# Latent attention on one core: full-column products issued as four 32-column tiles, transposes put last in each step

## The chip, the cores and the metric

The kernel runs on one core of one Trainium2 chip. The metric is device time in microseconds (us), as the median of several runs. Engines are named as in the profile: PE is the matrix engine, PEld its weight loads, DVE the vector engine, ACT the scalar engine, POOL GpSimd, SP the engine that issues most DMAs.

## What is computed

The input is 8 sequences of 1024 tokens with 256 features, all in float32. A latent attention comes first, then a feed-forward part of two layers of windowed attention and gated MLP; the change touches only the first. Cut to that, the reference is:

```python
# NH=16 heads of HD=16, DR=32 rope features, latent width D_C=128
x = layernorm(x)
c_kv   = x @ W_kv_down                        # 256 -> 128
k_rope = rotary(c_kv @ W_k_rope)              # 32, shared by the heads
k, v   = c_kv @ W_k_up, c_kv @ W_v_up         # 256 each
q      = x @ W_q
q_rope = rotary(x @ W_q_rope)
scores = (einsum(q, k) + einsum(q_rope, k_rope)[:, None]) / sqrt(HD + DR)
w      = softmax(causal(scores))
out    = x0 + (w @ v) @ W_o                   # x0: the input before layernorm
```

## The kernel before

**Tiling.** `mla` handles the 8 batches (sequences) one after another. Four heads are worked on together, as a group g of four 32-row slices of the array. The 512 queries of one half c against 128 keys kb of one group make a unit; small causal units are put together in pairs. There are 36 units in each batch, and the loop that starts at L545 (`mla`) takes one unit in each step, so a batch has 36 steps, numbered 0 to 35 below.

**One step.** In a step the loop does, in this order:

- `scores` (L391) of this step's unit. Its products have 32 rows and 128 columns of the array each (K=32), into two PSUM tiles `sc` of a pool with two buffers; then two exponentials on ACT (L407) turn them into `pt`.
- `turned` (L411) of the unit of the step before: two DVE multiplications (L421) by the exponential of the shared rope scores, `er`.
- `values` (L423) of the unit of two steps before. Its products have 128 rows and 32 columns (four heads side by side in four column tiles), into `acc`.
- `finished` (L444) if a group ended in the step before: four 128x128 transposes into `pst`, then a reciprocal and a product on DVE (L449, L450).
- `do(b, step)` (L529): what the table at L487 puts beside this step. These are the dense work of the next batch (normalising, `turn`, `down`, `rope_q`, `rope_k`, `query`, `keys`, `value`, `rotary`) and the end of this or the former one (`out_turn`, `out_add`). Entries read (step, whose batch, what).

**Shapes on the array.** All dense products go through `times` (L182) with all 128 rows and 128 columns; all transposes go through `flip` (L185), also 128x128. So PE works in three forms: 32x128 for scores, 128x32 for values, 128x128 for the rest. A float32 product shows as two matmul records and two weight loads in the trace.

**Order and buffers.** Inside `tc.manual_schedule` (L546) PE, DVE, ACT and POOL take their instructions in the order in which the program writes them. The results of `times` and `flip` share a PSUM pool `psum1` with two buffers (L167, tag `mm`); a result is read out by ACT or DVE, and its buffer then comes free. `query`, `down`, `rope_q` and `out_add` hold their buffer over two steps, since each step makes one half of the sum.

**After it.** The windowed attention (`local`, L577) begins when the last batch is done. Its loads are issued while the last batch still runs.

The loop around the change is:

```python
                    if done:
                        bt, e = done.pop(0)
                        bt.finished(*e)
                    done += ended
                    do(b, step)
```

Of the kernel before, what the change touches and what calls it, by code (L numbers as in the profile page):

```python
# [81 lines left out]
def preln_mla_local_kernel(  # L82
# [27 lines left out]
    nc = tc.nc  # L110
# [44 lines left out]
    def mla(ctx: ExitStack, verdict):  # L155
# [23 lines left out]
            return xt  # L179


        def times(out, w, rhs, start, stop):  # L182
            nc.tensor.matmul(out, w, rhs, start=start, stop=stop)  # L183

        def flip(out, t):  # L185
            nc.tensor.transpose(out, t, ident)
# [61 lines left out]
        class Batch:  # L248
# [51 lines left out]
            def dense(self, name, ws, rhs, n, c):  # L300

                if c == 0:
                    self.sums[name, n] = psum.tile([P, 512], F32, tag="mm", name=f"{name}{self.b}_{n}")
                ps = self.sums[name, n]
                times(ps, ws[c], rhs[c][:, HALF[n]], c == 0, c == len(ws) - 1)
                return self.sums.pop((name, n)) if c == len(ws) - 1 else None
# [43 lines left out]
            def value(self, g):  # L350
                self.v = vs[self.b % 2]
                ps = psum.tile([P, 512], F32, tag="mm", name=f"psv{self.b}_{g}")
                for i in range(2):
                    t = 2 * g + i
                    times(ps[:, i * D : (i + 1) * D], self.ckvT[:, t * P : (t + 1) * P], wv, True, True)
                on_v(
                    self.v[:, 2 * g : 2 * g + 2, : NH * VW].rearrange("p a (h d) -> p a h d", h=NH)[..., :HD],
                    ps.rearrange("p (a h d) -> p a h d", a=2, h=NH),
                )
# [12 lines left out]
            def rotary(self, c, kb):  # L372
                q0, w, er = self.block(c, kb)
                ps = psum.tile([P, 512], F32, tag="mm", name=f"psR{self.b}_{c}_{kb}")
                times(ps[:, :w], self.rk[:, kb * P : (kb + 1) * P], self.rq[:, q0 : q0 + w], True, True)
                n = 12 * self.b + 8 * (1 - c) + kb
                nc.scalar.activation(er, ps[:, :w], AF.Exp, scale=SCALE, accum_out=most[:, n : n + 1])
                nc.vector.tensor_reduce(least[:, n : n + 1], er, AX.X, ALU.min)  # L378
                if q0 == kb * P:
                    nc.gpsimd.affine_select(  # L380
                        out=er[:, :P], in_=er[:, :P], pattern=[[1, P]],
                        compare_op=ALU.is_ge, fill=0.0, base=0, channel_multiplier=-1,
                    )
# [100 lines left out]
        def at(step, who, name, *args):  # L484
            beside.setdefault(step, []).append((who, name, args))

        for step, who, *what in (  # L487
            (0, 1, "load"), (0, 0, "query", 1, 1, 0), (0, 0, "query", 1, 1, 1),
            (1, 0, "value", 2),
            (2, 0, "keys", 1, 0),  # L490
            (3, 0, "keys", 1, 1), (3, 1, "statistics", 0, 0),
            (4, -1, "out_turn", 0), (4, 0, "query", 0, 0, 0), (4, 1, "statistics", 0, 1),
            (5, 0, "query", 0, 0, 1), (5, -1, "out_turn", 2), (5, 1, "statistics", 1, 0),
            (6, -1, "out_add", 0, 0), (6, -1, "out_add", 0, 1),
            (7, -1, "out_add", 2, 0), (7, 1, "statistics", 1, 1),
            (8, -1, "out_add", 2, 1), (8, 0, "value", 3),
            (9, 0, "query", 1, 0, 0), (9, 1, "normalise", 0, 0),
            (10, 0, "query", 1, 0, 1), (10, 0, "rotary", 0, 3), (10, 1, "normalise", 0, 1),
            (11, 0, "rotary", 0, 0),
            (12, 0, "rotary", 0, 2), (12, 1, "turn", 0), (12, 1, "normalise", 1, 0),  # L500
            (13, 1, "down", 0, 0), (13, 1, "normalise", 1, 1),
            (14, 1, "down", 0, 1),
            (15, 0, "rotary", 0, 1),
            (16, 1, "turn", 1),
            (17, 1, "down", 1, 0),
            (18, 1, "down", 1, 1), (18, 1, "rope_q", 0, 0),
            (19, 1, "rope_q", 0, 1),
            (20, 1, "rope_q", 1, 0), (20, 1, "rope_k", 0),
            (21, 1, "rope_q", 1, 1),
            (22, 1, "rope_k", 1), (22, 1, "query", 0, 1, 0),  # L510
            (23, 1, "query", 0, 1, 1),
            (24, 1, "keys", 0, 0), (24, 1, "value", 0),
            (25, 1, "value", 1),
            (26, 1, "keys", 0, 1),
            (27, 1, "rotary", 1, 0),
            (28, 1, "rotary", 1, 1),
            (29, 1, "rotary", 1, 2), (29, 1, "rotary", 1, 7),
            (30, 0, "out_turn", 4), (30, 1, "rotary", 1, 3),
            (31, 1, "rotary", 1, 6), (31, 0, "out_add", 4, 0),
            (32, 0, "out_add", 4, 1), (32, 0, "out_turn", 6),  # L520
            (33, 1, "rotary", 1, 4),
            (34, 1, "rotary", 1, 5), (34, 0, "out_add", 6, 0),
            (35, 0, "out_add", 6, 1),
        ):
            at(step, who, *what)
# [3 lines left out]
        def do(b, step, only=(-1, 0, 1)):  # L529
            for who, name, args in beside.get(step, []):  # L530
                if who in only and 0 <= b + who < B:
                    getattr(batches[b + who], name)(*args)
# [13 lines left out]
        with tc.manual_schedule(engines={E.PE, E.DVE, E.Activation, E.Pool}):  # L546
            for b in range(B + 1):
                for step in range(len(units) if b < B else 9):
                    if b < B:
                        if step == 0:  # L550
                            batches[b].start()
                        line.append((batches[b], units[step], batches[b].scores(step, units[step])))
                    if len(line) > 1 or b == B:
                        for bt, unit, pts in line[-2 : -1] if b < B else line[-1:] if step == 0 else []:
                            bt.turned(unit, pts)
                    ended = []
                    if len(line) > 2 or b == B and line:
                        bt, unit, pts = line.pop(0)
                        ended = [(bt, e) for e in bt.values(unit, pts)]
                    if done:  # L560
                        bt, e = done.pop(0)
                        bt.finished(*e)
                    done += ended
                    do(b, step)

        ok = small.tile([P, 2, B * 12], F32, tag="okr", name="okr", bufs=1)
        nc.vector.tensor_scalar(ok[:, 0, :], most, TURN, None, ALU.is_le)
# [1016 lines left out]
    with ExitStack() as one:  # L1584
        mla(one, verdict)
# [91 lines left out]
```

## Time and profile before

| | |
|---|---|
| median of 3 runs | 3622.2 us (3621.33 to 3624.78) |
| the profiled execution: its own time | 3623.07 us |
| its span in the profile | 3621.2 us |
| latent attention, from the first scores to the last values | about 28.5 to 1053 us of the span |
| PE busy share of the span | 98% |
| DVE, ACT, POOL busy share | 62%, 50%, 37% |

In the timeline a line gives the start in us, the duration in us, the engine, the source line, the tiles it writes and reads, the array form (rows*columns), the shape and the number of records merged. Matmuls overlap in the trace: the end of one record lies after the start of the next. The time that one takes on the array is therefore read from start to start. In a list of one line's instructions, three durations in ns are the least, the median and the most.

### The profile page before, as it was taken

How to read it: one execution, taken by the hardware profiler on the slowest of the kernel's cores; microseconds unless marked ns; L12 is line 12 of the kernel's file. 1: busy time of each engine (PE TensorE's matmuls, PEld its weight loads, DVE VectorE, ACT ScalarE, POOL GpSimd, SP SyncE). 2: the span in 40 equal slices, each digit the busy share in tenths (PEclk: the TensorE clock that was granted, in tenths of full speed). 3: DMA queues.
4: the chain of work that ended last, by engine and by line, in shares of the span. 5: the costliest groups of instructions: out<-in, count | busy, mean ns of one | idle time of the engine just before them, and what ended most of it. 6: DMA issues, size and time to landing. Idle time of an engine off the chain costs nothing.

```text
span 3621.2 us, 77779 instructions
## 1 busy us (share of the span) xinstructions
PE 3556.6 (98%) x34338; PEld 2046.6 (57%) x34338; DVE 2246.5 (62%) x3273; ACT 1828.0 (50%) x2362; POOL 1348.9 (37%) x1031
## 2 busy tenths in 40 slices
PE   8999999999999999999999999999999999999999
PEld 3434443443345666666666666666666666666666
DVE  6888888888876545555555554555555555555543
ACT  5777777777653344444444444444444444444441
POOL 1001000100118545545454553545455454444530
PEclk9999999999999999999999999999999999999999
DMA  1000000000110000000010001111101110110011
GB/s 58 7 19 24 16 12 21 24 7 7 69 56 13 19 33 19 31 27 31 22 37 30 19 31 57 36 33 45 45 25 36 33 36 26 43 42 24 26 33 42
DMA packets 102838, 110.14 MB, mean 30 GB/s; under 512 B 12930, under 2 KB 87003, under 8 KB 102363
## 3 DMA queue, kind: packets, MB, share of 16 engines
q1 hardware_dynamic: 99354, 101.49, 8.8%
q8 instruction: 271, 4.44, 0.5%
q10 hardware_dynamic: 3136, 3.59, 0.3%
q14 instruction: 77, 0.62, 0.1%
HBM read 63.11 MB, written 41.94 MB: 29 GB/s over the span
## 4 chain that ended last, share of the span: by engine, by line
PE 90%; DVE 5%; ACT 3%; issue 1%; DMA 1%; POOL 0%; ACTq 0%; SPq 0%; DVEq 0%; POOLq 0%
PE ag L945 14%; PE pair L769 12%; PE psy L978 9%; PE sc L399 9%; PE acc L432 7%; PE psw L890 6%; PE o L862 6%; PE pv L796 6%; PE psq L810 3%; PE s L862 3%; PE pair L829 3%; DVE rs L869 2%; PE psq L183 2%; PE psR L183 2%; ACT pt L834 2%; PE psx L183 1%
## 5 line engine op out<-in xcount | busy, mean ns | idle before, releaser
L125 POOL TENSOR_TENSOR rn<-ss,half 128x16 f32<-128x16 f32 x128 | 372.1, 2907 | 1028.8 <-DVE ss L785 1028.8
L421 DVE TENSOR_TENSOR pt<-pt,er 128x1024 f32<-128x1024 f32 x576 | 678.3, 1224 | 6.9 <-ACT pt L407 6.7
L407 ACT ACTIVATE pt<-sc 128x1024 f32<-128x1024 f32 x576 | 558.9, 1023 | 244.1 <-PE sc L399 220.0
L945 PE MATMUL ag<-d,l 128*128 128x512 f32 x1408 | 641.3, 597 | 3.4 <-ACT qT L78 2.7
L769 PE MATMUL pair<-l_qkv,xT 128*128 128x512 f32 x1024 | 466.9, 599 | 3.7 <-ACT pt L834 2.0
L834 ACT ACT_TABLE_LOAD x120 | 154.0, 1283 | 620.4 <-PE pair L829 620.3
L945 PEld LDWEIGHTS ag<-d,l 128*128 128x128 f32 x1408 | 262.0, 190 | 311.7 <-issue 303.2
L776 DVE TENSOR_TENSOR t<-pair,l_cos 128x1024 f32<-128x1024 f32 x128 | 156.5, 1223 | 354.7 <-ACT sq L774 354.7
L399 PE MATMUL sc<-q,k 32*128 32x512 f32 (+3 forms) x3072 | 350.9, 524 | 7.4 <-ACT pt L407 7.0
L769 PEld LDWEIGHTS pair<-l_qkv,xT 128*128 128x128 f32 x1024 | 189.7, 191 | 237.6 <-issue 206.5
L869 DVE RECIPROCAL rs<-s 128x256 f32<-128x256 f32 x128 | 224.6, 1755 | 157.8 <-PE s L862 157.7
L954 DVE SCALAR_TENSOR_TENSOR hid<-ag,l_b,ge 128x512 f32<-128x512 f32 x160 | 120.2, 751 | 317.6 <-ACT ge L953 178.4
L380 POOL TENSOR_SCALAR_AFFINE_SELECT er<-er 128x128 f32<-128x128 f32 x64 | 62.7, 980 | 678.5 <-DVE least L378 678.5
L432 PE MATMUL acc<-pt,v 128*32 128x512 f32 (+3 forms) x3072 | 312.0, 500 | 1.9 <-DVE pt L421 1.9
L788 POOL TENSOR_TENSOR t<-t,t 128x1024 f32<-128x1024 f32 x128 | 306.4, 2394 | 0.0
L978 PE MATMUL psy<-l,hid 128*128 128x256 f32 x1280 | 297.1, 379 | 0.0
L774 ACT ACTIVATE sq<-pair 128x1024 f32<-128x1024 f32 x128 | 131.1, 1024 | 313.0 <-issue 218.8
L978 PEld LDWEIGHTS psy<-l,hid 128*128 128x128 f32 x1280 | 243.2, 190 | 46.7 <-issue 15.3
L862 PE MATMUL o<-pt,v 128*32 128x128 f32 x7680 | 260.1, 274 | 0.8 <-POOL pt L836 0.8
L862 PEld LDWEIGHTS o<-pt,v 128*32 128x32 f32 x7680 | 204.2, 110 | 85.7 <-issue 82.8
L834 ACT ACTIVATE pt<-pair 128x1024 f32<-128x1024 f32 (+1 forms) x256 | 234.7, 968 | 34.6 <-PE pair L829 33.3
L399 PEld LDWEIGHTS sc<-q,k 32*128 32x128 f32 x3072 | 141.0, 184 | 189.8 <-ACT pt L407 113.6
(132 smaller groups left out, 5188.4 us busy)
## 6 DMA issues: line engine op xcount, KB each, us to landing
y<-xs SPq DMA_DIRECT2D x128, 128.0 KB, 1.9
h<-y SPq DMA_DIRECT2D x32, 512.0 KB, 3.8
x<-in_L_attn_x_dram SPq DMA_DIRECT2D x16, 512.0 KB, 4.6
x2d<-x SPq DMA_DIRECT2D x32, 256.0 KB, 2.3
xs<-x2d SPq DMA_DIRECT2D x16, 512.0 KB
x<-x2d SPq DMA_DIRECT2D x16, 512.0 KB
xs<-xs SPq DMA_DIRECT2D x32, 256.0 KB, 2.6
xs<-xs SPq DMA_DIRECT2D x16, 512.0 KB, 5.4
```

The lines of the kernel that those rows point to most:

```text
L125: nc.gpsimd.tensor_tensor(out_, in_, half[:, :n], ALU.pow)
L399: nc.tensor.matmul(two[n // 2][:, n % 2, lo : lo + w], self.k[g][rows, kb * P : (kb + 1) * P], self.q[rows, g // 2, q0 : q0 + w], start=Tr ...
L407: nc.scalar.activation(pt, sc, AF.Exp, scale=SCALE)
L421: nc.vector.tensor_tensor(t, t, er.to_broadcast([P, 1024 // w, w]), ALU.mult)
L432: nc.tensor.matmul(self.acc[g][32 * n : 32 * n + 32, q0 - c * 512 :], self.v[:, kb, h * VW : h * VW + 32], pts[n // 2][:, n % 2, lo : lo + w],
L769: nc.tensor.matmul(qk[:, n].rearrange("p h d -> p (h d)"), self.left(i)[c], w["qkv"][:, c, n * INNER : (n + 1) * INNER], start=(c == 0), s ...
L788: nc.gpsimd.tensor_tensor(t1, t1, t2, ALU.add)
L834: nc.scalar.activation(pt[:, :, : n * P], flat[:, :, : n * P], AF.Exp, scale=-1.0)
L862: nc.tensor.matmul(o[rows, g, a, :] if a < 2 else s[rows, g, :], left if a < 2 else ones, pts[m][g][:, 2 * (j % 2) + j // 2, off : off + P ...
L869: nc.vector.reciprocal(rs, s)
L945: nc.tensor.matmul(ps, w["1"][:, c, i, :], d[:, c, :], start=(c == 0), stop=(c == 1))
L978: nc.tensor.matmul(ps[:, t, :], left, w["2"][:, i, :], start=(i == 0), stop=(i == NF))
```

## The change

`times` cuts its product into four column tiles of 32, one after another, each with its own 32 columns of the weights and its own 32 output partitions. The right side is the same for all four. `flip` stays as it is. In the loop `do(b, step)` comes before `finished`, so the dense products follow directly after `values`, and the transposes of `finished` come last in the step. In the table three pairs of entries change places, so that transposes (`out_turn`, `turn`) come after the other entry of their step.

```diff
+        QUARTER = [slice(32 * n, 32 * n + 32) for n in range(4)]
+
         def times(out, w, rhs, start, stop):
-            nc.tensor.matmul(out, w, rhs, start=start, stop=stop)
+            for four in QUARTER:
+                nc.tensor.matmul(out[four], w[:, four], rhs, start=start, stop=stop)
...
-            (4, -1, "out_turn", 0), (4, 0, "query", 0, 0, 0), (4, 1, "statistics", 0, 1),
+            (4, 0, "query", 0, 0, 0), (4, -1, "out_turn", 0), (4, 1, "statistics", 0, 1),
...
-            (12, 0, "rotary", 0, 2), (12, 1, "turn", 0), (12, 1, "normalise", 1, 0),
+            (12, 0, "rotary", 0, 2), (12, 1, "normalise", 1, 0), (12, 1, "turn", 0),
...
-            (30, 0, "out_turn", 4), (30, 1, "rotary", 1, 3),
+            (30, 1, "rotary", 1, 3), (30, 0, "out_turn", 4),
...
+                    do(b, step)
                     if done:
                         bt, e = done.pop(0)
                         bt.finished(*e)
                     done += ended
-                    do(b, step)
```

## The prediction

> **What bounds the kernel now.** I read the busy shares first, then the stage's window, then the timeline of a few steps on PE and ACT, then the durations of single instructions. PE leads everywhere, and in one whole batch of the stage (the fourth, 415.52 to 531.82 us, 36 steps) it has next to no idle time, with DVE second:
>
> ```profile
> PE 3556.6 (98%) x34338; PEld 2046.6 (57%) x34338; DVE 2246.5 (62%) x3273; ACT 1828.0 (50%) x2362; POOL 1348.9 (37%) x1031
> ```
> ```profile
> 415.52:531.82 116.30, 115.57 (x853) 46.01 (x852) 100.41 (x132) 84.59 (x115) 9.35 (x8) 1.00 0.05 17
> 982.80:997.10 14.30, 8.27 (x33) 1.53 (x34) 9.63 (x25) 5.07 (x6) 2.65 (x4) 0.72 0.77 274
> ```
>
> The columns after the length are PE, PEld, DVE, ACT, POOL; so DVE is at 100.4 of 116.3 and ACT at 84.6. But busy PE is not useful PE: the time lies in the changes of form. The timeline of PE:
>
> ```profile
> 482.04 1.14 PE L399 MATMUL sc<-q,k 32*128 32x512 f32 x8
> 483.11 1.06 PE L432 MATMUL acc<-pt,v 128*32 128x512 f32 x8
> 484.11 1.13 PE L183 MATMUL psrq<-xnT,wqr 128*128 128x512 f32 x2
> 485.16 1.17 PE L399 MATMUL sc<-q,k 32*128 32x512 f32 x8
> 486.26 1.07 PE L432 MATMUL acc<-pt,v 128*32 128x512 f32 x8
> 487.26 1.12 PE L183 MATMUL psrq<-xnT,wqr 128*128 128x512 f32 x2
> 488.22 1.02 PE L183 MATMUL psrk<-ckvT,wkr 128*128 128x512 f32 x2
> 489.18 1.14 PE L399 MATMUL sc<-q,k 32*128 32x512 f32 x8
> ```
>
> In step 19 (482.04 to 485.16) there are three blocks of two passes, eight records of four tiles at a time for scores and values and two records for the dense product. Inside a run of one form a 512-column record follows the one before after 429 ns (0.427 us of streaming and 2 ns), so two passes are 0.85 us. The blocks last 1.07, 1.00 and 1.05. The rest is of two kinds. The first weight load after a change of form is not hidden, which the durations show:
>
> ```profile
> L183 PE MATMUL psrq<-xnT,wqr x64: 592/592/697, 19.4 to 872.0; 128*128 128x512 f32 x64
> L186 PE MATMUL pst<-ident,oaT x256: 272/273/475, 86.7 to 1054.6; 128*128 128x128 f32 x128
> ```
>
> 697 - 592 = 105 ns for a dense product, 106 for scores (692 against 586), 25 for values (617 against 592), and 59 for the transposes of pst (from start to start). The other is the change itself. From starts of single records, less streaming and exposed load: scores to values 111 ns, values to full form 116, full form back to scores 95. The same to 2 ns in nearly all changes of the batch.
>
> ACT sets a second limit. In the same steps:
>
> ```profile
> 483.22 1.94 ACT L407 ACTIVATE pt<-sc 128x1024 f32<-128x1024 f32 x2 [1.34 <-PE sc L399]
> 486.34 1.94 ACT L407 ACTIVATE pt<-sc 128x1024 f32<-128x1024 f32 x2 [1.18 <-PE sc L399]
> ```
>
> Scores of step 19 start at 482.04, the exponentials at 483.22, and they end at 485.16; their PSUM tiles are the ones that the scores of step 20 need. The third tile of step 20 started at 485.208, 37 ns after the second. So **no step can be shorter than about 3.12 us**, even if PE is ready.
>
> **What the Trainium skill says.** "TensorEngine Tiling (Array Packing)", Key Properties: "Changing tiling mode (not just tile) drains the TensorE"; the trace agrees, with 95 to 116 ns a change. "TensorE: Matmul & The Clock Gate", LDWEIGHTS (loading the stationary operand), puts a load at its columns over 1.2 in ns, 107 for 128 and 27 for 32; the exposed 105 and 25 above agree (the load's own record lasts 189 and 109). The same page, Measured speedup vs the span model, lets column tiles run together at about 4 ns from tile to tile; the four value tiles start 6 to 7 ns apart. That page, Part 1, also calls DVE and ACT strict first-in first-out, on which the DVE working below rests.
>
> **The change part by part.**
>
> *Four tiles for one.* The value products are the very form that `times` takes on: 128 rows, 32 columns, four at a time. Their passes follow each other at streaming time plus 2 or 3 ns, at 512, 384, 256 and 128 columns. So a dense product costs the same in four tiles as in one. What the trace lacks is four tiles that read one and the same right side: bound 0 to 25 ns a pass (an exposed 32-column load each time); reading one address cannot stream faster. I take 0, since the rate of four different right sides, the harder case, is seen. That 5,568 more matmul records are issued I put at 0 too: values of 128 columns already issue 16 records in 0.21 us.
>
> *The change of form.* Before, a step with dense work pays 116 + 106 + 95 = 317 ns round it. After, the products go on in the form of `values` (no exposed load) and then change to scores; values straight to scores happened cleanly a few times in the last batch, at 114 to 116 ns. Saved: 317 - 116 = **0.20 us** in each step that has products and no transposes. Those are 23 of the 36: all but 1, 2, 4, 5, 12, 14, 15, 16, 27, 28, 30, 32, 33. In those with transposes nothing is saved if a transpose came first before, and 106 - 59 = 0.05 if a product did (5 and 12).
>
> *Where it lands.* Of the 23, twelve (3, 7, 9, 11, 13, 17, 19, 21, 23, 25, 26, 35) last 3.12 to 3.19 us now and stand at the ACT limit: PE would be ready 0.2 earlier and then wait in front of the third score tile. They gain nothing alone, since their neighbours are PE-bound from that tile on; only 25 and 26, one after the other, let one 0.2 through. The other eleven (0, 6, 8, 10, 18, 20, 22, 24, 29, 31, 34) last 3.35 to 4.02, with the exponentials done 0.23 to 0.90 us ahead of the next third tile: full gain, as far as DVE follows.
>
> *The transposes moved.* PE runs the same four of them. DVE's reciprocal and product (0.25 and 0.42, 0.68 together) now stand behind what `do` gave DVE, and `turned` of the next step stands behind them. The margin of `turned` before the values that read it was, in the step after next: over 1.2 us from steps 1, 2, 14 and 32; 0.53 from 15; 0.64 from 27; 0.50 from 28; 0.92 from 33. At 15 the rope product ends 0.66 earlier and its exponential 0.35 earlier, so 0.2 of margin is left. At 27 and 28 not: DVE's work for pst (512.52 to 513.23, while it waited for `er` until 514.28) now comes after the minimum, at 514.9 to 515.6. The pair for step 29 ends at 517.9 instead of 517.23, the values want it at 517.87: 0.1 late. The next finish adds its 0.7: the pair for step 30 ends at 521.4 instead of 520.72, so values start at 521.5 instead of 521.22. The 0.2 of step 29 is lost, and 0.28 more; 31 gives 0.2 back. Steps 29 to 31 together: **-0.08**.
>
> *Table swaps.* Step 32: `out_turn` stood 0.60 us for `onat`, written by the DVE work of pst (L450 ends 531.12, its first transpose starts 531.27). It now comes before that; pst then waits for the addition of psx instead, to about 531.15, and the next scores start about 0.14 earlier. Step 4 and 5: query now takes its buffer before `out_turn` 0. If buffers rotated strictly, `out_turn` 2 would need the one that query has just filled. I take it that the one freed first is given: in step 32 pso began at 531.27, before the reader of psx was done (531.72), so it was not given the buffer next in turn. Price if wrong: query is read at 3.0 to 3.6 after the step's start, transposes start there and not at 2.92, 0.69 a batch. Step 3 gains 0.05, as keys of step 2 are read out earlier; step 12 gains 0.07 (its rope exponential comes earlier), step 5 0.05. Normalise and `turn` are on different engines: 0. No queue of SP or POOL is passed; the x2d stores follow their additions.
>
> *Sum.* A batch in the middle: 9 steps (0, 6, 8, 10, 18, 20, 22, 24, 34) and the pair, 10 x 0.20 = 2.0; 0.05 + 0.05 + 0.07 + 0.14 - 0.08 = 0.23; **2.23**. Six such: 13.4. The first has no former batch (0, 6, 8, 3, 5 fall out): 1.4 + 0.13 = 1.5. The last has no next one; after step 11 it stands on ACT and on DMAs: 0, 6, 8, 10 and 0.1, 0.9. In the dense work before the first unit and in the closing steps, form now changes some five times more, about 0.2 each: 1. Net 13.4 + 1.5 + 0.9 - 1 = **about 15 us**. Against the profiled execution 3623.07 - 15 = 3608.1; it was 0.9 above the median, so 3622.2 - 15 = **3607**.
>
> **Rivals.** *More:* the ACT limit gives way (the first two score tiles start early, exponentials follow) and all short steps gain: 11 x 0.2 x 7 = 15 more, 3592. Against it: the third tile is already seen waiting. *Buffer:* strict turns in step 5, 7 x 0.69 = 5 less: 3612. *Hand-over:* at 982.8 to 997.1 PE is busy 8.3 of 14.3 us, since ACT waits 8.1 us for the scale loads queued among its exponentials. Where those stand may move; another such wait beside the buffer case gives about 3620, no visible change. *Slower:* DVE. If `turned` comes late after each of the 8 finishes by the whole 0.7, a batch loses 5.6 and gains 2.7, +2.9 x 7.5 = 22: 3644. It decides where margins are under 0.7; I see three such of eight, and with four at 0.7 (2.8) gain and loss are even.
>
> **Numbers.** Forecast 0.62 (3599 to 3615 by itself), more 0.10, buffer 0.10, hand-over 0.08, slower 0.10. This kernel's measurement tells about 0.2%, 7 us, from no change. Faster: 0.58 + 0.10 + 0.08 = 0.76; same: 0.04 + 0.02 + 0.06 + 0.01 = 0.13; slower: 0.02 + 0.09 = 0.11. The 25 ns bound on a pass (116 passes a batch, half on the path, 11 us) lies inside. Range 3595 to 3622: it leaves out most of *more*, and *slower*.
>
> **What would show it.** Right: no 128*128 form at L183's products; the first of them after acc without 105 ns; short steps still 3.12 us with PE waiting for ACT's pt; steps 20, 22, 24 at 3.81; a batch of 114.1 us; acc of step 30 waiting for DVE. Wrong: passes over 429 ns in `times`, short steps under 3.0, or values waiting for DVE in many steps.

## The result, and the profile after it

| | before | after |
|---|---|---|
| median of 5 runs | 3622.41 us (3621.33 to 3624.78) | 3604.68 us (3603.06 to 3608.34) |
| ratio, 95% interval | | 0.9951 (0.9937 to 0.9966) |
| profiled execution: its own time, its span | 3623.07, 3621.2 us | 3604.27, 3602.5 us |
| one batch in the middle of the stage | 126.75 us | 124.54 us |

The change gains 17.7 us, where 15 were forecast. First the busy shares of the page of the kernel after, then the windows of its fourth batch (length, then PE, PEld, DVE, ACT, POOL): its first 33 steps, and the whole of it.

```profile
PE 3536.6 (98%) x37122; PEld 2029.3 (56%) x37122; DVE 2240.3 (62%) x3273; ACT 1826.7 (51%) x2362; POOL 1344.5 (37%) x1031
```
```profile
409.06:523.56 114.50, 113.77 (x1169) 44.83 (x1165) 99.10 (x130) 85.22 (x117) 9.57 (x8) 1.00 0.05 18
409.06:533.60 124.54, 123.81 (x1300) 49.72 (x1296) 108.21 (x142) 92.02 (x127) 11.09 (x10) 1.00 0.05 18
```

PE's busy share still reads 98%. It loses 20 us of busy time while it executes 2,784 more matmul records, so the share couldn't have told whether there was anything to gain.

The prediction has an error in its reading of the window: from 415.52 to 531.82 us are steps 0 to 32, thus 33 steps and not the 36 of a batch. The whole batch of the kernel before is this window:

```profile
415.52:542.26 126.74, 126.01 (x949) 51.34 (x948) 109.12 (x141) 92.22 (x126) 11.78 (x10) 1.00 0.05 18
```

No sum rests on it, as the steps were added one by one. But the "batch of 114.1" to look for took the gain of 36 steps, 2.23 us, from the length of 33. The same 33 take 114.50 us now, 1.80 less; the other 0.40 us of the batch's gain lie in steps 34 and 35, outside that window. The 5,568 records more are also twice what the page counts as matmuls: half of them are weight loads.

The timeline of PE after, steps 19 to 21, the same steps that were shown of before:

```profile
474.48 1.14 PE L403 MATMUL sc<-q,k 32*128 32x512 f32 x8
475.55 1.07 PE L436 MATMUL acc<-pt,v 128*32 128x512 f32 x8
476.43 1.04 PE L187 MATMUL psrq<-xnT,wqr 128*32 128x512 f32 x8
477.40 1.37 PE L403 MATMUL sc<-q,k 32*128 32x512 f32 x8
478.70 1.07 PE L436 MATMUL acc<-pt,v 128*32 128x512 f32 x8
479.58 1.04 PE L187 MATMUL psrq<-xnT,wqr 128*32 128x512 f32 x8
480.44 1.04 PE L187 MATMUL psrk<-ckvT,wkr 128*32 128x512 f32 x8
481.41 1.14 PE L403 MATMUL sc<-q,k 32*128 32x512 f32 x8
```

From values to dense product it is now 0.88 us (475.55 to 476.43) and not 1.00: no change of form, no first load. From product to scores 0.97 and not 1.05. Together 0.20 us. Step 19 lasts 2.92 us from scores to scores, and step 20 lasts 4.01 as before. The block of scores in step 20 shows why: 1.37 us long, where those of steps 19 and 21 take 1.14. In it the first two tiles start at 477.40, the third and the fourth at 477.64; those two write the second `sc` tile, which the second exponential of step 19 still reads. ACT in the same steps:

```profile
475.65 1.94 ACT L411 ACTIVATE pt<-sc 128x1024 f32<-128x1024 f32 x2 [1.31 <-PE sc L403]
478.57 1.94 ACT L411 ACTIVATE pt<-sc 128x1024 f32<-128x1024 f32 x2 [0.99 <-PE sc L403]
```

The exponentials of step 19 end at 477.59, and the third tile starts 0.05 us after that. So the 0.20 us that PE has ready in step 19 stand in front of the third tile, inside step 20.

The durations of single instructions, as before (least, median, most in ns):

```profile
L187 PE MATMUL psrq<-xnT,wqr x256: 592/592/593, 20.2 to 857.4; 128*32 128x512 f32 x128
```

Of before, the longest product with `wqr` had 697 ns. No exposed load is left on it. And ACT's wait in the last batch, where the loads of the scales stand among its exponentials, before and after (in all, how often, longest, in us):

```profile
ACT pt L407 <- DMA l_fsin<-in_L_ffn_q_scale_dram: 8.1, 1, 8.1
ACT pt L411 <- DMA l_fsin<-in_L_ffn_q_scale_dram: 5.9, 1, 5.9
```

Its shortening by 2.2 us is not a gain of that size: by the starts of scores the whole hand-over returned only about 0.4 us.

Where the 18.7 us of the span come from, by the starts of scores in both traces:

| stretch | gain, us | forecast |
|---|---|---|
| dense work at the start, to the fourth score product of the first unit | -0.46 | part of "ends", -1 together |
| first batch, from there | 2.48 | 1.5 |
| batches 2 to 7 (2.2 each) | 13.30 | 13.4 |
| last batch, to its step 17 | 0.94 | 0.9 |
| last batch, from there to its last scores (hand-over among it) | 0.54 | 0 |
| last scores to the first product of the windowed attention (0.86 of it the granted clock) | 1.01 | part of "ends" |
| windowed attention and what follows | 0.92 | 0 |

The last line says nothing of the change: this stretch took 2558.8 to 2562.5 us in the kernels of this study, whose code there is the same, and 0.92 us lie within that spread. And 0.86 us of the line before it are no saved changes of form. The last values of the batch wait for DVE in both kernels, but in the profiled execution of before they then run at a granted clock of 0.54 (the number behind POOL), and after at 1.00. First before, then after:

```profile
1050.40:1053.40 3.00, 2.97 (x16) 0.71 (x16) 1.11 (x1) 0.00 (x0) 0.00 (x0) 0.54 0.14 51
```
```profile
1033.60:1035.80 2.20, 1.87 (x17) 0.58 (x17) 1.11 (x1) 0.00 (x0) 0.00 (x0) 1.00 0.19 69
```

Their last passes of 384 columns follow each other after 0.64 us before and 0.32 after. From the last scores to the first transposes behind the values it is 9.07 us in four of the eleven profiles of this study (the three kernels with the old order, and the one with tiles of 64 columns), and 8.21 to 8.28 in the seven others. There is one profile of each kernel, so whether the new order has a part in the clock isn't shown, and I count it to neither part.

### The profile page after: what moved, and what is told of

Same layout as the page of the kernel before. It is cut to its first block, busy times and chain, and to the rows that moved or that the text cites. A ratio compares the mean times of both kernels' runs of the same rounds, so it can differ in the third digit from the quotient of the medians.

```text
span 3602.5 us, 83361 instructions
## 1 busy us (share of the span) xinstructions
PE 3536.6 (98%) x37122; PEld 2029.3 (56%) x37122; DVE 2240.3 (62%) x3273; ACT 1826.7 (51%) x2362; POOL 1344.5 (37%) x1031
## 4 chain that ended last, share of the span: by engine, by line
PE 89%; DVE 4%; ACT 4%; issue 1%; DMA 1%; POOL 0%; ACTq 0%; SPq 0%; DVEq 0%; POOLq 0%
PE ag L949 14%; PE pair L773 12%; PE psy L982 9%; PE sc L403 9%; PE acc L436 7%; PE psw L894 6%; PE o L866 6%; PE pv L800 6%; PE psq L814 3%; PE s L866 3%; PE pair L833 3%; DVE rs L873 2%; ACT pt L838 2%; PE psq L187 2%; PE psR L187 2%; PE psx L187 1%
## 5 line engine op out<-in xcount | busy, mean ns | idle before, releaser
L403 PE MATMUL sc<-q,k 32*128 32x512 f32 (+3 forms) x3072 | 367.2, 525 | 6.2 <-ACT pt L411 6.0
L403 PEld LDWEIGHTS sc<-q,k 32*128 32x128 f32 x3072 | 157.7, 184 | 168.5 <-ACT pt L411 106.4
```

The source lines that it names most:

```text
L403: nc.tensor.matmul(two[n // 2][:, n % 2, lo : lo + w], self.k[g][rows, kb * P : (kb + 1) * P], self.q[rows, g // 2, q0 : q0 + w], start=Tr ...
```

## The experiments

My theory: the gain is the change of form saved at products that follow values; it shows in full only where a step, or a pair of neighbours, is above ACT's limit of two scores and two exponentials; the new order costs DVE a little in steps 29 to 32. Rivals: the order brings the gain and the tiles don't; the narrower stationary tile as such is quicker; the loss of the short steps is PE's and not ACT's.

**Four tiles alone.** The kernel before with the loop over `QUARTER` in `times`; order and table as they were:

```diff
         def times(out, w, rhs, start, stop):
-            nc.tensor.matmul(out, w, rhs, start=start, stop=stop)
+            for four in QUARTER:
+                nc.tensor.matmul(out[four], w[:, four], rhs, start=start, stop=stop)
```

> The kernel before with the four column tiles alone; the order in a step and the table stay as they were. Form-change theory: steps with products and no transposes gain as in the changed kernel, about 2.0 us a batch; the steps in which transposes stand between values and products (1, 2, 4, 14, 15, 27, 28, 30, 33) now change form once more, about 0.15 us each, 1.3 in all; DVE keeps its old order, so the values of step 30 are not late. A batch (36 steps) of about 125.4 us against 126.7 before, in all about -10 us, 3612. Rival A, the tiles do it all: 3605. Rival B, the order does it all: no change, 3622.

Measured: 3613.36 us (3611.13 to 3614.67) against 3623.29, ratio 0.9971 (0.9959 to 0.9982); a batch takes 125.61 us. The tiles bring about 1.1 of the 2.2 us of a batch, near the forecast. Steps with transposes pay: 1, 2, 27, 28, 30 and 33 are each 0.14 us longer than before the change, as transposes and products were one form and are now two.

**Order alone.** The kernel after with `times` as it was:

```diff
-            for four in QUARTER:
-                nc.tensor.matmul(out[four], w[:, four], rhs, start=start, stop=stop)
+            nc.tensor.matmul(out, w, rhs, start=start, stop=stop)
```

> The changed kernel with full-column products again: only the order in a step and the table are changed. Form-change theory: products in the full form cost what they did, transposes behind them change no form; the values of step 30 are late for DVE. A batch of 126.7 to 127.1 us, 3622 to 3625 in all. Rival, the order is worth most: under 3612.

Measured: 3624.79 us (3624.06 to 3625.98), ratio 1.0004 (0.9995 to 1.0013); 127.12 us a batch, 0.37 more than before. By itself the order is worth nothing; with full columns it puts the dearer first load (106 ns against 59) after the values, 0.05 us in each step with transposes. It pays only because the tiles make product and values one form: two parts of which one gains 10 us, the other nothing, and both together 18.

**Two tiles of 64 columns.** The kernel after with

```diff
-        QUARTER = [slice(32 * n, 32 * n + 32) for n in range(4)]
+        QUARTER = [slice(64 * n, 64 * n + 64) for n in range(2)]
```

> The changed kernel with two tiles of 64 columns instead of four of 32. Form-change theory: 128x64 is a fourth form, so products after values change form again (116 ns, and an exposed load of about half of 106), and transposes after them once more: 23 steps gain 0.03 to 0.05 of which half reach the path, 12 lose about 0.17; a batch of about 128.4 us, 3635 in all. Rival, narrower tiles help by themselves (shorter loads): between the two kernels, 3605 to 3615.

Measured: 3627.65 us (3625.14 to 3631.89), ratio 1.0012 (1.0006 to 1.0019); 127.41 us a batch. The timeline of PE of this kernel, one step (19):

```profile
483.55 1.14 PE L403 MATMUL sc<-q,k 32*128 32x512 f32 x8
484.62 1.06 PE L436 MATMUL acc<-pt,v 128*32 128x512 f32 x8
485.61 1.08 PE L187 MATMUL psrq<-xnT,wqr 128*64 128x512 f32 x4
486.62 1.22 PE L403 MATMUL sc<-q,k 32*128 32x512 f32 x8
```

From values to product it is 0.99 us, with a first load of some 53 ns and a change of 114 to 116 ns. So narrower tiles don't help as such: it must be the very form of the neighbour. Direction as expected, the size not (3635 us expected): the price of a transpose's step, 0.15 us, came as worked out, but at 8 or 9 steps of a batch and not at 12.

**A lower ACT limit.** To see whether ACT holds the short steps, the second exponential of each unit works on 512 columns, as the expectation says, and the values read other tiles in place of the missing one:

```diff
-                    nc.scalar.activation(pt, sc, AF.Exp, scale=SCALE)
+                    nc.scalar.activation(pt[:, : 2 - i], sc[:, : 2 - i], AF.Exp, scale=SCALE)
...
-                for pt in pts:
+                for pt in (pts[0], pts[0]):
...
-                            self.v[:, kb, h * VW : h * VW + 32], pts[n // 2][:, n % 2, lo : lo + w],
+                            self.v[:, kb, h * VW : h * VW + 32], pts[n // 2][:, n % 2 if n < 2 else 0, lo : lo + w],
```

> The changed kernel with less work for ACT: the exponential of the fourth head of each group is left out (the second exponential covers 512 columns and not 1024, the values of that head take the third head's), and the second multiplication on DVE runs on the first pair again, so that DVE has the same work; the output is not the reference's. ACT-limit theory: the third score tile no longer waits, steps 0, 4, 8, 10, 14, 20, 22, 24, 26 lose the 0.2 us that they took back after a short step; a batch of about 122.5 us against 124.5, in all about -17 us, 3588. Rival, the time taken back is PE's own: no change, 3605.

Measured: 3580.16 us (3579.23 to 3581.67), ratio 0.9882 (0.9866 to 0.9899); 121.42 us a batch. The timeline of PE in this kernel, and of ACT beside it:

```profile
467.79 1.14 PE L403 MATMUL sc<-q,k 32*128 32x512 f32 x8
468.86 1.06 PE L436 MATMUL acc<-pt,v 128*32 128x512 f32 x8
469.74 1.04 PE L187 MATMUL psrq<-xnT,wqr 128*32 128x512 f32 x8
470.71 1.14 PE L403 MATMUL sc<-q,k 32*128 32x512 f32 x8
```
```profile
468.96 1.51 ACT L411 ACTIVATE pt<-sc 128x1024 f32<-128x1024 f32 x2 [2.27 <-PE sc L403]
```

The exponentials end at 470.47, ahead of the next scores, and the block at 470.71 is again 1.14 us long and not 1.37. Long steps behind short ones fall from 4.01 to 3.78 us, short ones stay at 2.93. PE's work on the path is the same, so the 0.2 us did wait for ACT. That the gain is 3.1 us a batch and not the expected 2.0 is in steps for which I had not counted ACT or DVE as a limit: 12 (4.18 to 4.00), 17 and 18 together (6.94 to 6.71), 30 (3.86 to 3.57) and 32 (4.71 to 4.41).

**DVE in step 30.** The rope term's minimum, which stands on DVE in front of the division behind the transposes and of `turned`'s two multiplications (the pair), is put into a list and issued after `finished`:

```diff
-                nc.vector.tensor_reduce(least[:, n : n + 1], er, AX.X, ALU.min)
...
+                later.append((n, er, q0 == kb * P))
...
+                    minima()
```

> The changed kernel with the minimum of rotary (and the mask behind it) issued at the end of the step, after finished: DVE gets its old order back, PE and ACT are as changed. DVE-order theory: the values of step 30 are on time again, step 30 is 3.5 us and not 3.86; a batch of about 124.2 us against 124.5, in all -2.5 us, 3602. Rival, step 30 is late for something else: no change, 3605.

Measured: 3602.89 us (3599.64 to 3604.23) against 3624.93 before it, ratio 0.9942 (0.9926 to 0.9959); 124.18 us a batch. As a whole it can't be told from the kernel after (0.9951), but a batch can: 124.54 to 124.18. In the trace of after, step 30 shows DVE on the path (DVE, PE and PE's weight loads together):

```profile
510.65 2.35 DVE L425 TENSOR_TENSOR pt<-pt,er 128x1024 f32<-128x1024 f32 x2
512.70 1.19 PE L436 MATMUL acc<-pt,v 128*32 128x256 f32 x14
513.05 0.36 PEld L436 LDWEIGHTS acc<-pt,v 128*32 128x32 f32 x10 [0.21 <-DVE pt L425]
513.59 0.60 PE L187 MATMUL psR<-rq,rk 128*32 128x512 f32 x2
...
513.72 0.39 PE L436 MATMUL acc<-pt,v 128*32 128x256 f32 x2
```

The pair ends at 513.00, and the tiles of values that read it start only then. With the minimum moved back (PE):

```profile
508.59 1.16 PE L398 MATMUL sc<-q,k 32*128 32x384 f32 x16
509.68 1.07 PE L431 MATMUL acc<-pt,v 128*32 128x256 f32 x16
510.57 1.04 PE L187 MATMUL psR<-rq,rk 128*32 128x512 f32 x8
511.54 0.66 PE L190 MATMUL pso<-ident,onat 128*128 128x128 f32 x4
512.12 1.14 PE L398 MATMUL sc<-q,k 32*128 32x512 f32 x8
```

The values are one unbroken block of 16, and step 30 lasts 3.54 us, not 3.86. DVE's new order costs 0.36 us a batch, nearly all in this step, and the forecast named the place.

**The addition of step 32.** Its `out_add` goes to step 31, and the rotary of step 31 to step 25:

```diff
-            (25, 1, "value", 1),
+            (25, 1, "value", 1), (25, 1, "rotary", 1, 6),
...
-            (31, 1, "rotary", 1, 6), (31, 0, "out_add", 4, 0),
-            (32, 0, "out_add", 4, 1), (32, 0, "out_turn", 6),
+            (31, 0, "out_add", 4, 0), (31, 0, "out_add", 4, 1),
+            (32, 0, "out_turn", 6),
```

> The changed kernel with the second half of the output sum moved from step 32 to 31 and rotary 6 from step 31 to 25. Buffer theory for step 32: the transposes of finished no longer stand for the addition that reads psx, 0.69 us; nothing else changes. A batch of about 123.8 us against 124.5, in all -5 us, 3599.5. Rival, another wait takes its place (the DVE chain is late anyway): under 0.2 us a batch, 3604.

Measured: 3599.4 us (3596.5 to 3601.64), ratio 0.9931 (0.9914 to 0.9947); 123.91 us a batch, 0.63 less. Steps 31 and 32 in the kernel after (ACT, DVE and PE), from the exponentials of step 31 on:

```profile
516.71 1.94 ACT L411 ACTIVATE pt<-sc 128x1024 f32<-128x1024 f32 x2 [0.53 <-ACT oT L78]
...
519.00 0.41 ACT L381 ACTIVATE er<-psR 128x256 f32<-128x256 f32 x1
...
519.53 0.42 DVE L382 TENSOR_REDUCE least<-er 128x1 f32<-128x256 f32 x1 [0.53 <-ACT er L381]
519.87 2.45 DVE L425 TENSOR_TENSOR pt<-pt,er 128x1024 f32<-128x1024 f32 x2
...
521.79 0.66 PE L190 MATMUL pso<-ident,onat 128*128 128x128 f32 x4
522.24 0.68 DVE L481 TENSOR_TENSOR x<-psx,x 128x512 f32<-128x512 f32 x1
...
522.97 0.66 PE L190 MATMUL pst<-ident,oaT 128*128 128x128 f32 x4 [0.53 <-DVE x L481]
523.56 0.50 PE L403 MATMUL sc<-q,k 32*128 32x256 f32 x4
```

The transposes of pst wait until the addition has read the buffer that they take: it ends at 522.92, they start at 522.97, 0.69 us later than they could have followed pso. With the addition in step 31, step 32 of that kernel ends so (PE):

```profile
518.97 0.60 PE L190 MATMUL pst<-ident,oaT 128*128 128x128 f32 x4
519.50 1.21 PE L403 MATMUL sc<-q,k 32*128 32x256 f32 x16
```

Step 32 takes 3.10 us, not 4.71, and step 31 takes 3.80, not 3.37: 1.18 less. Steps 25 to 27 take 0.49 more together, with the rotary that came there, and step 33 takes 0.06 more. The rest, 0.63, is what the batch gains.

**Steps filled to the limit.** If ACT's limit is what keeps the short steps' 0.2 us, then moving work from a long step into its short neighbour must set it free. The dense products are cut into parts of 256 columns and dealt by the table; the core of it:

```diff
-                times(ps, ws[c], rhs[c][:, HALF[n]], c == 0, c == len(ws) - 1)
+                for u in range(lo, hi):
+                    h, c = divmod(u, len(ws))
+                    cols = slice(256 * h, 256 * h + 256)
+                    times(ps[:, cols], ws[c], rhs[c][:, HALF[n]][:, cols], c == 0, c == len(ws) - 1)
...
-            (19, 1, "rope_q", 0, 1),
-            (20, 1, "rope_q", 1, 0), (20, 1, "rope_k", 0),
+            (19, 1, "rope_q", 0, 2, 4), (19, 1, "rope_q", 1, 0, 1),
+            (20, 1, "rope_q", 1, 1, 2), (20, 1, "rope_k", 0, 0, 2),
```

> The changed kernel with the dense products cut into parts of half the columns and dealt out so that steps 3, 7, 9, 11, 13, 17, 19, 21, 23 and 35, which stood at 2.92 us of PE work, get about 3.36 and their neighbours less; the same work in all, with 256-column passes in place of 512. ACT-limit theory: no step is under 3.12, so PE no longer waits for the exponentials: 0.2 us at nine places, and the wait of the second psn in step 12 goes too (0.36): about -2.1 us a batch, 122.4, in all -15 us, 3590. Rival, the short steps were not held by ACT: no change or the cost of more weight loads, 3605 to 3610.

Measured: 3587.48 us (3587.18 to 3588.92), ratio 0.99 (0.9883 to 0.9917); 122.18 us a batch. The timeline of PE, step 22:

```profile
476.06 1.14 PE L415 MATMUL sc<-q,k 32*128 32x512 f32 x8
477.13 1.07 PE L448 MATMUL acc<-pt,v 128*32 128x512 f32 x8
478.02 0.61 PE L187 MATMUL psrk<-ckvT,wkr 128*32 128x256 f32 x8
478.45 1.05 PE L187 MATMUL psq<-xnT,wq 128*32 128x256 f32 x16
479.42 1.15 PE L415 MATMUL sc<-q,k 32*128 32x256 f32 x16
```

The step takes 3.36 us, the scores are 1.14 long. Steps 7 to 9 and 18 to 24 now take 3.36 to 3.37 each, two of them 6.73; in the kernel after such a pair took 2.93 + 4.01 = 6.94, before 3.12 + 4.01 = 7.13. So a pair saves the full 2 x 0.20 on PE, and the kernel after got half of it.

**The same filling without the change.** The kernel before, with its products cut and dealt likewise:

> The kernel before, with full-column products and its old order, but with the products cut and dealt out as in the filled kernel. ACT-limit theory: before, a short step's PE work was 3.12 us itself and ACT's limit lay just on it, so filling has little to win here: some 0.03 us at nine places and the second psn's wait in step 12 (0.46), about -0.7 us a batch, 126.0, in all -5.5 us, 3618. Rival, filling is worth as much by itself as it was on the changed kernel (17 us): 3606.

Measured: 3620.92 us (3618.18 to 3621.69) against 3623.44, ratio 0.9992 (0.9984 to 1.0); 126.10 us a batch. Here a pair takes 2 x 3.56 = 7.12 us, as long as unfilled, since there PE and ACT stood at the same 3.12 in a short step. Filling returns 2.4 us of the kernel after's batch and 0.65 of the kernel before's, nearly all of that in steps 11 and 12. In all it gains 2.5 us and not the 5.5 expected; the batches are as expected, but in the profiled execution the second one begins 1.36 us later than in the kernel before. ACT's limit was no loss before the change: the change made it one.

**All together.** Minimum last, addition earlier, steps filled, on top of the change.

> The last three together: filled steps, minimum last, addition earlier. If the three waits are separate, their gains add up: about -3.1 us a batch, 121.4, in all -23 us, 3582. If they are one and the same slack seen three times: 3590, as with filled steps alone.

Measured: 3581.32 us (3581.15 to 3582.67), ratio 0.9883 (0.9866 to 0.9899); 121.20 us a batch. That is 3.34 us less a batch than after; the three alone add up to 0.36 + 0.63 + 2.36 = 3.35. They are three separate losses, and this is the quickest version of the study that leaves nothing out: 1.2% under the kernel before, of which the change as it was made is 0.5%.

## Why the prediction was right, and where its steps were off

**The price of a form change: right.** A step with dense products and no transposes loses 0.20 us on PE: one change of form (95 ns) and one exposed first load (106 ns). Changes that the kernel before hardly showed came as put: values straight to scores 114 to 116 ns. Four tiles that read one right side follow each other at streaming time plus 2 to 3 ns; of the 0 to 25 ns a pass, 0 was the right choice. This agrees with "Mode switching requires drain" of the Trainium skill ("TensorEngine Tiling (Array Packing)", Key Properties); the price is in the traces only.

**The short steps: right as a sum, wrong in what would show it.** The forecast was that a short step gains nothing alone and its long neighbour 0.20 us. By first scores it is the other way round: 3.12 to 2.93 for the short one, 4.01 to 4.01 for the long. The first two score tiles write buffers that are free early and go ahead; only the third waits, and by then the next step has begun. The sum of the pair is as forecast, 6.94. By the letter of "what would show it" (short steps at 3.12, none under 3.0, long ones at 3.81) the mechanism would have been called wrong. A step in which a wait stands behind the second of four tiles has to be measured from the third, or in pairs. Shortening ACT's work and filling the steps both show that the limit is real, and so the rival *more* (11 more steps gain) is out.

**The buffer: right.** Step 5 takes 3.51 us (3.56 before), so `out_turn` 2 was not held by query's buffer. In the trace its transposes start at 429.69 us, and ACT begins to read query's result only at 429.83. No strict turns.

**The order on DVE: right in place, in size nearly.** Steps 29 and 30 together lose 0.17 us; the forecast was a loss of 0.28, with step 31 giving 0.2 back: -0.08. The rival *slower* (eight late finishes) did not come: with DVE's old order back only step 30 (by 0.32 us) and step 29 (0.04) get shorter.

**The term that failed: steps 31 and 32.** The forecast was that step 31 returns 0.20 and step 32 gains 0.14, thus 0.34. Together they gained 0.09: step 31 did give its 0.20, and step 32 lost 0.11. The two gains could not be added. The wait of pst for the addition ends a chain that hangs on the scores of step 31: its exponentials, a copy and the rope exponential follow each other on ACT, then the minimum, the pair and the addition on DVE (the lines are shown at the addition of step 32). From those scores (515.49) to the end of the addition (522.92) it is 7.43 us. The time of 531.15 that I had put for that end in the trace before is 7.48 us behind the scores of step 31 there (523.67), so the chain was sized rightly. What was wrong is to let step 31 bring its end forward too: where step 31 is shorter, step 32 waits longer for the same end. Two runs bear this out. With the order alone step 31 is 0.20 us longer than after, and the chain is 7.49 us. With the shorter exponential, which is a link of the chain, step 32 takes 0.30 less. For steps 29 to 32 that makes -0.09 and not +0.06.

**What made up for it: small terms, too low.** Steps 3 and 4 give 0.09 (0.05 forecast), 11 and 12 together 0.14 (0.07), 17 and 18 together 0.23, which I had counted as one 0.20. These are 0.15 more than forecast, and steps 29 to 32 were 0.15 less. So 2.21 a batch beside 2.23 is partly luck. The first batch gained 2.48 for 1.5: the steps 2, 5, 8 and 9, which I had let fall out or put at nothing, gain there too. In the last batch 0.94 to step 17 is what was put. The hand-over moved (8.1 to 5.9 us) and yet returned some 0.4: at step 20, right behind the wait, the scores are 1.7 us further ahead of those of the kernel before than at step 17 (17.98 against 16.26), at step 22 only 0.2 (16.49), and from step 25 on 0.4 (16.68). The *hand-over* rival had the place, but as a gain, not a loss.

**The ends: put too dear.** I put -1 for more changes of form in the dense work at the start and in the closing steps. The start costs 0.46. The closing gains 1.01, of which 0.86 is the granted clock: from the last scores to the first transposes behind the values it was 9.07 us (1044.345 to 1053.414) and is 8.21 (1027.547 to 1035.755), while DVE's last pair ends 7.16 us behind those scores in both. Without it the ends cost 0.3 together (0.46 less 0.15), and not 1.

So the forecast of 15 stood at 17.7 for the reason it gave; in the span the difference is the first batch, the ends, and 1.8 us that the saved changes of form don't explain: 0.86 of clock and 0.92 of the stage behind.

## What to carry to other kernels

Where short matmul blocks of several array forms take turns, count changes of form and exposed first loads per step, and ask whether one operation can be issued in its neighbour's form; then order the step so that equal forms touch. Before adding up the savings, find in each step which second engine stands close behind: what is set free in a step at that limit is kept only if work can be moved into it from a longer step, and this dealing may be worth more than the change. Measure such steps in pairs or from the instruction that waits, not from the step's first.

## What the runs showed of the hardware that I had not expected

Column tiles run ahead of each other. In step 30 after, the values that wait for DVE's pair run until their last pass begins at 513.72, and yet the next product's first tiles (psR, other columns) start at 513.59, ahead of it. The Trainium skill has this as a property ("TensorEngine Tiling (Array Packing)", Key Properties: "Tiles operate independently"), and this trace agrees. In the run with the order alone the product takes all columns, and it starts only behind a change of form after the last value tile: 523.24 to 523.55.

The change of form has nearly one price, when it is read from the right tile. From the first tile of the last pass before it, as the prediction reads it, it seems to depend on the form that is left: 110 to 117 ns where that has four tiles, 102 to 104 with two tiles of 64 columns, 95 to 97 with one. But the tiles of a pass start 6 to 7 ns after each other. From the start of the last tile, less streaming, it is 95 to 97 ns out of `128*32`, `128*64` and `128*128` alike, and 90 to 93 out of `32*128`, nearly everywhere in the traces of before, after, four tiles alone and tiles of 64 columns. On top comes the first load of the next form: 106 ns at 128 columns, 57 to 59 for transposes, about 53 at 64 columns, 25 at 32. Why the transposes, of 128 columns too, show only 57 to 59 is open. So a full-column product between values and scores costs 317 ns in changes and first load, where four tiles of 32 columns cost 116.
